# A decoder layer on one core: weight sums moved in GpSimd's order, routers taken in pairs, and four smaller moves

## The chip, the core and the metric

The kernel runs on one core of a Trainium2 chip. The engines run side by side, each in the order of its own queue: TensorE (PE in the profile; PEld is its loading of weights), VectorE (DVE), ScalarE (ACT), GpSimd (POOL), and SyncE (SP), which here only issues DMAs. ScalarE issues DMAs too. The metric is device time in microseconds (us). Lower is better.

## The reference

x has shape (32, 64, 512), so there are 2048 tokens of 512 elements, seen as 16 tiles of 128 tokens; ctx_1024 is (32, 64, 128). Everything is in 32-bit floats.

```python
x = x + attn(layernorm(x))        # 32 heads of 128, rmsnorm on q and k, with weights and biases
x = x + xattn(layernorm(x), ctx)  # 64 channels: q, k, v, skip are 64x64 products
x = x + ffn(layernorm(x))         # router of 64 experts, the top 8, expert biases

# ffn
logits = einsum('th,eh->te', flat, router_weight) + router_bias      # 512 -> 64
scores = softmax(logits);  topk_w, topk_idx = top_k(scores, 8)
w_sum = topk_w.sum(-1);    w_dense = zeros(T, 64) with topk_w at topk_idx
out = flat * w_sum + w_dense @ expert_bias                           # 64 -> 512
```

In the attention the sequence is 64 tokens long for each of 32 rows, and its weights Wq, Wk, Wv are 512 x 4096, Wo is 4096 x 512.

## The kernel before

**Products by Strassen.** The big products are made of seven block products instead of eight, at one level or two. For this, sums of blocks are wanted on both sides. *Weights* (`Weights.sums`, L114 to L127; `more_sums`, L129 to L155): two VectorE or GpSimd subtractions t1, t2 (768 columns, L120), then two more on GpSimd, then for the second level four of 512 and four of 384 columns (L152 to L155). It is a generator with a `yield` after each of the four portions. `sums_of_next(n)` starts it for the weights of the next group, and each `make(1)` runs one portion, always on GpSimd. *Tokens* (`AttentionInput.turn`, L339; `inner_input`, L368): VectorE adds L372 and L373, GpSimd adds L375 and L376.

**The attention's loop.** 32 groups (n = 0 to 31) are 16 pairs of heads (hg) times two halves of the tokens. For hg = 0 (n = 0 and 16) a group is two `single` units, one after the other, because the second level's token sums aren't there yet; each runs through the steps of `HeadGroup.project`, and a dictionary from step to function says what is issued behind which step. All other groups are one `Window` of two units, with a plan of 4 x 4 places (n, m), to which `more` adds. Behind step 6 and step 11 of a single unit, and at set places of a window, `line.scale` multiplies earlier queries and keys by fetched inverse roots: the key part at once on GpSimd (L572), the query part a little later on VectorE (L574). `line.attend` then makes the scores s (L585), which need both, and the mixtures o.

**Order.** TensorE follows the order of the program text everywhere; VectorE, ScalarE and GpSimd follow it too during the attention. So an instruction that is issued earlier in the text stands ahead of all that follow on its engine. After the attention a scheduler places the instructions of those three engines, while TensorE's order stays as written. PSUM tiles rotate: three for projections (`ps_a`), two for transposes and values (`ps_t`), three for scores, keys and router logits (`ps_s`).

**The tail.** The output product goes through the tiles in pairs of a Strassen step (`strassen_out`), in chunks of eight TensorE passes. After each chunk `advance()` moves the tiles on that wait for cross attention and experts, each a generator (`after_attention`) whose `yield k` says how many chunks to let pass. `cross_attention` loads the context (L1090), makes keys and values `kv` (L1094, L1095), energies `e` (L1105), probabilities, their transposes and `py` (L1114, L1149). `experts` makes the transposed input `ft`, the logits `pl` (L1173), the largest eight and the dense weights `wds` on VectorE, the transposed weights `pw`, and the mixtures `pm` (L1222), added at L1225. Two tiles share `pw` and the mixtures already; each has its own logits. `layernorm` (L266) takes the inverse root on GpSimd, except for the last tile's, which ScalarE makes.

**Other lines touched.** `normed_tile` (L1326) normalises a tile of the second half in three steps, of which the third is VectorE's L1328 and a store. `load_wo` (L846) loads blocks of Wo; for the first of them two go through SP's queue ahead of the last window, and two through ScalarE's at place (1, 0).

Of the kernel before, what the change touches and what calls it, by code (L numbers as in the profile page):

```python
# [13 lines left out]
P = 128  # L14
# [27 lines left out]
def decoder_layer(  # L42
# [202 lines left out]
    def fill_behind(t, what):  # L245
        if (t, what) in FILL:
            fill(FILL[t, what])

    def statistics(xs, name, on_gpsimd=False):

        n = len(xs)
        mv = small.tile([P, n, 2], F32, tag=f"mv{n}", name=f"mv_{name}")
        for i, xt in enumerate(xs):
            st = small.tile([P, 6], F32, tag="st", name=f"st{i}_{name}")
            nc.vector.bn_stats(st, xt)
            nc.vector.bn_aggr(mv[:, i, :], st)
        rstd = small.tile([P, n], F32, tag=f"rs{n}", name=f"rs_{name}")
        if on_gpsimd:
            nc.gpsimd.tensor_scalar(rstd, mv[:, :, 1], LN_EPS, None, ALU.add)
            nc.gpsimd.tensor_tensor(rstd, rstd, mhalf[:, 0:n], ALU.pow)  # L260
        else:
            nc.scalar.activation(rstd, mv[:, :, 1], AF.Ln, bias=ln_eps)
            nc.scalar.activation(rstd, rstd, AF.Exp, scale=-0.5)
        return [(mv[:, i, 0:1], rstd[:, i : i + 1]) for i in range(n)]

    def layernorm(xt, name):  # L266
        ((mean, rstd),) = statistics([xt], name, not name.endswith(str(NT - 1)))
        xn = work.tile([P, D], F32, tag="xn", name=f"xn_{name}", bufs=3)
        nc.vector.tensor_scalar(xn, xt, mean, rstd, ALU.subtract, ALU.mult)
        return xn  # L270
# [572 lines left out]

    def load_wo(k, n, places, queue):  # L846

        halves = []
        for i, it in enumerate(places):
            it = it.rearrange("p (g f) -> p g f", f=DH)  # L850
            queue.dma_start(
                out=it,
                in_=wo.rearrange("(g k p) f -> k p g f", k=HG, p=HD)[
                    k, :, i * KH : (i + 1) * KH, bass.ts(n, DH)
                ],
            )
            halves.append(it)
        return halves
# [225 lines left out]
    def cross_attention(t, xt, apart):  # L1084
# [2 lines left out]

        name = f"x{t}"
        ct = work.tile([P, MCTX], F32, tag="ct", name=f"ct_{t}")
        nc.sync.dma_start(out=ct, in_=ctx_flat[bass.ts(t, P), :])  # L1090
        xn = layernorm(xt, name)
        yield 1
        kv = ps_s.tile([P, 2, MCTX], F32, tag="ps", name=f"kv_{t}")
# [68 lines left out]
    def experts(t, xt):  # L1162
        name = f"f{t}"
        xn = layernorm(xt, name)

        yield 8 if t == NT - 2 else 3
        ft = work.tile([P, KC, P], F32, tag="ft", name=f"ft_{name}", bufs=1)
        nc.scalar.copy(ft, transposed(xn.rearrange("p (kc k) -> p kc k", k=P), name))
        fill_behind(t, "router's input")
        yield 1  # L1170
        pl = ps_s.tile([P, NEXP], F32, tag="ps", name=f"pl_{name}")
        for kc in range(KC):
            nc.tensor.matmul(  # L1173
                pl, ft[:, kc, :], rwt[:, kc, :], start=kc == 0, stop=kc == KC - 1
            )
        fill_behind(t, "router")
        lg = work.tile([P, NEXP], F32, tag="lg", name=f"lg_{name}")
        nc.vector.tensor_tensor(lg, pl, rb_b, ALU.add)
        top = small.tile([P, 8], F32, tag="top", name=f"top_{name}")
        nc.vector.max(top, lg)  # L1180
        neg = small.tile([P, 1], F32, tag="neg", name=f"neg_{name}")
        nc.vector.tensor_scalar(neg, top[:, 0:1], -1.0, None, ALU.mult)
        ex = work.tile([P, NEXP], F32, tag="ex", name=f"ex_{name}")
        den = small.tile([P, 1], F32, tag="den", name=f"den_{name}")
        nc.scalar.activation(ex, lg, AF.Exp, bias=neg, accum_out=den)
        inv = small.tile([P, 1], F32, tag="inv1", name=f"inv1_{name}")
        nc.vector.reciprocal(inv, den)

        rest = work.tile([P, NEXP], F32, tag="rest", name=f"rest_{name}")
        nc.vector.match_replace(rest, top, lg, -3e38)  # L1190
        chosen = work.tile([P, NEXP], F32, tag="chosen", name=f"chosen_{name}")
        nc.vector.tensor_tensor(chosen, lg, rest, ALU.not_equal)

        alone = t >= NT - 2
        side = 0 if alone else t % 2
        if side:
            wds, other = chosen_by.pop(t - 1)
        else:
            wds = work.tile([P, 2, NEXP], F32, tag="wds", name=f"wds_{name}")
        wd = wds[:, side, :]  # L1200
        nc.vector.scalar_tensor_tensor(wd, ex, inv, chosen, ALU.mult, ALU.mult)
        ws = small.tile([P, 1], F32, tag="ws", name=f"ws_{name}")
        nc.vector.tensor_reduce(ws, wd, AX.X, ALU.add)

        nc.vector.scalar_tensor_tensor(xt, xn, ws, xt, ALU.mult, ALU.add)
        if not alone and not side:
            chosen_by[t] = wds, xt
            return
        yield 3
        n = NEXP if alone else 2 * NEXP  # L1210
        pw = ps_t.tile([P, P], F32, tag="pt", name=f"pw_{name}")
        nc.tensor.transpose(pw[0:n, :], wds.rearrange("p a e -> p (a e)")[:, 0:n], ident)
        wt = work.tile([P, P], F32, tag="wt", name=f"wt_{name}")
        nc.scalar.copy(wt[0:n, :], pw[0:n, :])
        fill_behind(t, "weights")
        yield 1

        both = [(t, xt)] if alone else [(t - 1, other), (t, xt)]
        pms = [ps_a.tile([P, D], F32, tag="pa", name=f"pm{i}_{name}") for i in range(len(both))]
        for i, pm in enumerate(pms):  # L1220
            rows = slice(i * NEXP, (i + 1) * NEXP)
            nc.tensor.matmul(pm, wt[rows, :], eb_sb[rows, :], start=True, stop=True)  # L1222
        fill_behind(t, "experts")
        for (at, it), pm in zip(both, pms):
            nc.vector.tensor_tensor(it, it, pm, ALU.add)  # L1225
            nc.sync.dma_start(out=out_flat[bass.ts(at, P), :], in_=it)

# [150 lines left out]
    def make(count):  # L1378
        for _ in range(count):
            if making and next(making[0], making) is making:  # L1380
                making.pop()

    for n, (hg, half) in enumerate(groups):
# [3 lines left out]
        if hg == 0:  # L1387
# [2 lines left out]
                {  # L1390
                    3: lambda: coming[0].norm(),
                    6: lambda: (coming.pop(0).turn(), coming[0].norm()),
                    11: lambda: coming.pop(0).turn(),
                },
            )
# [7 lines left out]
            def inner(o):  # L1403
                next(inners[o], None)

            sums_of_next(n)
            make(1)
            single(
                units[1],
                {  # L1410
# [3 lines left out]
                    4: lambda: inner(5),  # L1414
                    6: lambda: (make(1), inner(2)),
                    8: lambda: inner(6),
                    11: lambda: make(2),
                    12: lambda: inner(7),
                },
            )  # L1420
        else:
            more = {
                (0, 3): [lambda n=n: sums_of_next(n), lambda: make(1)],
                (1, 0): [lambda: make(1)],
                (1, 3): [lambda: make(1)],
                (3, 0): [lambda: make(2)],
            }

            def also(n, m, it):
                more.setdefault((n, m), []).append(it)  # L1430
# [11 lines left out]
                    also(*at, lambda o=o: inner(o))  # L1442
            if half == 0 and 2 <= hg < 2 + NT // 2:
                norm = normed_tile(NT // 2 + hg - 2)
                for at in ((0, 0), (0, 3), (1, 2)):
                    also(*at, lambda norm=norm: next(norm, None))
            if (hg, half) == (NHG - 1, 0):

# [7 lines left out]

            if n + 1 == len(groups):
                four = four_blocks("wo_0")
                wo_b = [[load_wo(0, 0, four[0:2], nc.sync)], []]
                also(1, 0, lambda: wo_b[1].append(load_wo(1, 0, four[2:4], nc.scalar)))  # L1460
                a_0 = [[None, None], [None, None]]

                def mixture(t, h, place):
                    a_0[t][h] = load_mixed(t, h, place())

                def qk_buffer(name):
                    return work.tile([P, BLK], F32, tag="qk", name=name, bufs=4)
# [177 lines left out]
```

## Time and profile before

| | |
|---|---|
| median of 3 runs | 1870.45 us (1868.06 to 1873.12) |
| profiled execution | 1869.75 us |
| its span | 1868.0 us (1.75 us around it) |
| granted TensorE clock | 0.999 |
| busy: PE, PEld, DVE, ACT, POOL | 1850.4, 1616.9, 1245.1, 653.6, 1014.7 us |
| PE p_w L685 (second-level projections) | 721.1 us in 2940 passes |
| POOL L120 (first-level weight sums) | 249.7 us in 126 |

The profile is one execution. A timeline line gives the start, the time, the engine, the source line, the operation with what it writes and reads, and in brackets the idle time ahead of it with what ended it. A line of the waits gives who waited for whom, the sum, the number of times and the longest. A product of 32-bit floats shows as two passes of TensorE; a pass's own duration overlaps the next one's, so passes are costed by the distance of their starts.

### The profile page before, as it was taken

Reading aid. Unit: us, or ns where it says so; the run is one execution under the profiler, and the core shown is the slowest. Engines: PE = TensorE matmul, PEld = TensorE weight load, DVE = VectorE, ACT = ScalarE, POOL = GpSimd, SP = SyncE. Lnnn points to the kernel's source line nnn. Section 1 sums busy time; section 2 is a strip of 40 time slices with the busy share of each in tenths; the row PEclk is TensorE's granted clock in tenths of the full one; section 3 lists DMA queues with packets and bytes.
Section 4 is the critical chain, followed back from the end, with each engine's and each line's share of the span. In section 5 each row is a group of like instructions: output and inputs, shape, how many; then the busy total and the mean of one; then the engine's idle time right before and its main releaser. Section 6 shows DMA issues by size and latency. Waiting matters only on the chain.

```text
span 1868.0 us, 40676 instructions
## 1 busy us (share of the span) xinstructions
PE 1850.4 (99%) x16914; PEld 1616.9 (87%) x16914; DVE 1245.1 (67%) x2110; ACT 653.6 (35%) x1577; POOL 1014.7 (54%) x852
## 2 busy tenths in 40 slices
PE   9999999999999999999999999999999999999999
PEld 8888998898899888898889988988888888788876
DVE  6877777777666758777667767766684445554555
ACT  2344444444433443434443343444312202221222
POOL 4866777776667639776667777766242121212120
PEclk9999999999999999999999999999999999999999
DMA  4234434433443343333343333334944231223100
GB/s 143 69 122 144 134 125 131 131 109 110 131 136 114 114 139 112 109 109 103 130 134 123 109 110 114 103 115 141 312 122 159 91 116 68 71 94 116 46 26 23
DMA packets 164650, 215.06 MB, mean 115 GB/s; under 512 B 10161, under 2 KB 135153, under 8 KB 160369
## 3 DMA queue, kind: packets, MB, share of 16 engines
q1 hardware_dynamic: 157648, 206.62, 34.2%
q10 hardware_dynamic: 6816, 5.83, 1.0%
q8 instruction: 133, 2.18, 0.5%
q14 instruction: 53, 0.43, 0.1%
HBM read 172.05 MB, written 40.37 MB: 114 GB/s over the span
## 4 chain that ended last, share of the span: by engine, by line
PE 88%; DVE 4%; DMA 3%; POOL 3%; ACT 1%; issue 1%; SPq 0%; ACTq 0%; POOLq 0%; DVEq 0%
PE p_w L685 32%; PE py L879 17%; PE va L417 11%; PE vb L417 8%; PE o L622 3%; PE s L585 3%; PE ms_w L821 3%; PE pt_p L279 1%; PE pa L475 1%; PE e_x L1105 1%; PE py_x L1149 1%; PE pt_x L279 1%; POOL w L120 1%; PE pl_f L1173 1%; PE py_x L1114 1%; PE pb L475 1%
## 5 line engine op out<-in xcount | busy, mean ns | idle before, releaser
L685 PE MATMUL p_w<-x,w 128*128 128x256 f32 x2940 | 721.1, 382 | 2.5 <-DVE qk L696 1.7
L685 PEld LDWEIGHTS p_w<-x,w 128*128 128x128 f32 x2940 | 521.4, 190 | 59.3 <-DVE qk L696 1.2
L417 PEld LDWEIGHTS va<-w,x 128*128 128x128 f32 x2048 | 268.6, 192 | 13.0
L696 DVE TENSOR_TENSOR qk<-p_w,qk 128x512 f32<-128x512 f32 x360 | 213.1, 599 | 94.6 <-PE p_w L685 92.3
L433 ACT COPY v<-va 128x256 f32<-128x256 f32 x256 | 96.2, 376 | 497.5 <-PE va L417 497.5
L417 PE MATMUL va<-w,x 128*128 128x128 f32 x2048 | 269.9, 275 | 0.0
L709 DVE TENSOR_TENSOR qk<-p_w,qk 128x512 f32<-128x512 f32 x360 | 220.5, 620 | 46.5 <-PE p_w L685 43.1
L120 POOL TENSOR_TENSOR w<-w 128x768 f32<-128x768 f32 x126 | 249.7, 1993 | 2.4
L572 POOL TENSOR_TENSOR qk<-qk,rs 128x512 f32<-128x512 f32 x128 | 173.0, 1352 | 111.8 <-DMA rs<-row_w 99.4
L295 POOL TENSOR_TENSOR prob<-prob,inv 128x512 f32<-128x512 f32 x64 | 79.2, 1237 | 281.5 <-DVE inv L294 278.3
L879 PE MATMUL py<-wo,a 128*128 128x256 f32 x992 | 227.2, 382 | 0.0
L386 ACT ACTIVATE sq<-qk 128x512 f32<-128x512 f32 x256 | 161.4, 631 | 183.6 <-DVE qk L709 64.4
L879 PEld LDWEIGHTS py<-wo,a 128*128 128x128 f32 x992 | 184.1, 190 | 32.9 <-issue 8.6
L417 PEld LDWEIGHTS vb<-w,x 128*128 128x128 f32 x1536 | 201.3, 192 | 9.7
L417 PE MATMUL vb<-w,x 128*128 128x128 f32 x1536 | 202.4, 275 | 0.0
L574 DVE SCALAR_TENSOR_TENSOR qk<-qk,gqk,rs 128x512 f32<-128x512 f32 x128 | 164.7, 1287 | 3.8 <-DMA rs<-row_w 3.5
L879 PE MATMUL py<-wo_t,a 128*128 128x256 f32 x672 | 155.1, 382 | 0.0
L879 PEld LDWEIGHTS py<-wo_t,a 128*128 128x128 f32 x672 | 124.3, 190 | 18.2 <-issue 1.6
L1003 POOL TENSOR_TENSOR x<-x,p 128x256 f32<-128x256 f32 x42 | 42.9, 1043 | 166.7 <-ACT p L1056 72.2
L437 DVE TENSOR_TENSOR v<-vb,v 128x256 f32<-128x256 f32 x192 | 80.9, 421 | 57.0 <-ACT v L433 28.8
L765 POOL TENSOR_TENSOR qk<-qk 128x256 f32<-128x256 f32 x120 | 102.8, 857 | 10.5 <-DVE qk L709 5.8
L287 DVE TENSOR_REDUCE mx<-s 128x8 f32<-128x512 f32 x64 | 44.1, 689 | 85.4 <-PE s L585 85.3
(197 smaller groups left out, 2253.7 us busy)
## 6 DMA issues: line engine op xcount, KB each, us to landing
rs<-row_w SPq DMA_DIRECT2D x120, 512.0 KB
mixed<-ot SPq DMA_DIRECT2D x64, 512.0 KB
a<-mixed SPq DMA_DIRECT2D x32, 1024.0 KB
w<-in_wq_dram SPq DMA_DIRECT2D x64, 256.0 KB
w<-in_wk_dram SPq DMA_DIRECT2D x62, 256.0 KB
w<-in_wv_dram SPq DMA_DIRECT2D x62, 256.0 KB
x<-in_x_dram SPq DMA_DIRECT2D x20, 256.0 KB
rs<-row SPq DMA_DIRECT2D x8, 512.0 KB
```

The lines of the kernel that those rows point to most:

```text
L120: on.tensor_tensor(*(it.rearrange("p c j d -> p (c j) d") for it in (out, a, b)), ALU.subtract)
L386: nc.scalar.activation(sq, of, AF.Square)
L417: nc.tensor.matmul(to[:, j, :], left[i][:, c, j, :], right[i][:, c, 2, :], start=first and j == 0 and c == 0, stop=c == 1, skip_group_chec ...
L433: nc.scalar.copy(self.v[h, ab], what)
L437: nc.vector.tensor_tensor(it, what, it, ALU.add)
L572: nc.gpsimd.tensor_tensor(k, k, rk, ALU.mult)
L574: lambda: nc.vector.scalar_tensor_tensor(q, q, gqk, rq, ALU.mult, ALU.mult)
L685: nc.tensor.matmul(bank[:, s, :], self.w.inner[o][i], inner_x[self.half, o][i], start=first and s == 0, stop=True, skip_group_check=True,)
L696: nc.vector.tensor_tensor(to(t, j), bank, add(t, j), ALU.add)
L709: nc.vector.tensor_tensor(to(t, j), bank, to(t, j), ALU.add)
L765: on.tensor_tensor(to, to, what, ALU.add)
L879: nc.tensor.matmul(py, a[:, g, :], b[g // KH][:, g % KH, :], start=n == 0 and g == 0, stop=n == last and g == NHG - 1,)
```

## The change

1. In the single units, `sums_of_next(n)` and the first `make(1)` move from between the units to step 9 of unit 0, and `make(2)` (the 384-column sums, and the end of the generator) from step 11 of unit 1 to step 9.
2. In the windows of hg = 1 (n = 1 and 17) the four `make` places move from (0,3), (1,0), (1,3), (3,0) to (1,3), (2,1), (2,3), (3,1). Other windows keep theirs.
3. For hg = 2 the third step of `normed_tile` moves from (1,2) to (2,2).
4. The routers of tiles 0 to 13 are taken in pairs. Both inputs lie in one tile `fts`; the router's weights are now the stationary operand, 64 columns for each of the two tiles in turn, and the logits of both come out transposed in `plt`; ScalarE copies them to `lgt` and one transpose makes `pl` for both. VectorE adds the bias for both in one instruction, and then makes the two tiles' weights one after the other. Tiles 14 and 15 stay alone, as before.
5. The inverse root of x13, x15 and f15 is made by ScalarE (before: x15 and f15).
6. The contexts of tiles 0 and 1 are loaded through ScalarE's queue.
7. The first four blocks of Wo are all loaded through ScalarE's queue, one at each of (0,2), (1,0), (1,2), (1,3) of the last window.

```diff
+    on_scalar = (f"x{NT - 3}", f"x{NT - 1}", f"f{NT - 1}")
+
     def layernorm(xt, name):
-        ((mean, rstd),) = statistics([xt], name, not name.endswith(str(NT - 1)))
+        ((mean, rstd),) = statistics([xt], name, name not in on_scalar)
...
-        nc.sync.dma_start(out=ct, in_=ctx_flat[bass.ts(t, P), :])
+        (nc.scalar if t < 2 else nc.sync).dma_start(out=ct, in_=ctx_flat[bass.ts(t, P), :])
...
+        alone = t >= NT - 2
+        if alone or t % 2 == 0:
+            fts = work.tile([P, 2, KC, P], F32, tag="att", name=f"ft_{name}", bufs=1)
+        else:
+            fts, x_a, xn_a = chosen_by.pop(t - 1)
+        ft = fts[:, 0 if alone else t % 2, :, :]
...
+        elif t % 2 == 0:
+            chosen_by[t] = fts, xt, xn
+            return
         else:
...
+            tiles = [(t - 1, x_a, xn_a), (t, xt, xn)]
+
+            plt = ps_s.tile([P, P], F32, tag="ps", name=f"plt_{name}")
+            for kc in range(KC):
+                for side in range(2):
+                    nc.tensor.matmul(
+                        plt[side * NEXP : (side + 1) * NEXP, :],
+                        rwt[:, kc, :],
+                        fts[:, side, kc, :],
+                        start=kc == 0,
+                        stop=kc == KC - 1,
+                    )
+            lgt = work.tile([P, P], F32, tag="wt", name=f"lgt_{name}")
+            nc.scalar.copy(lgt, plt)
+            yield 0
+            pl = ps_s.tile([P, 2, NEXP], F32, tag="ps", name=f"pl_{name}")
+            nc.tensor.transpose(pl.rearrange("p a e -> p (a e)"), lgt, ident)
...
-        yield 3
-        n = NEXP if alone else 2 * NEXP
+        yield 3 if alone or t == 1 else 2
+        n *= NEXP
...
                     6: lambda: (coming.pop(0).turn(), coming[0].norm()),
+                    9: lambda n=n: (sums_of_next(n), make(1)),
                     11: lambda: coming.pop(0).turn(),
...
-            sums_of_next(n)
-            make(1)
...
                     8: lambda: inner(6),
-                    11: lambda: make(2),
+                    9: lambda: make(2),
                     12: lambda: inner(7),
...
+            at = ((0, 3), (1, 0), (1, 3), (3, 0)) if hg > 1 else ((1, 3), (2, 1), (2, 3), (3, 1))
             more = {
-                (0, 3): [lambda n=n: sums_of_next(n), lambda: make(1)],
-                (1, 0): [lambda: make(1)],
-                (1, 3): [lambda: make(1)],
-                (3, 0): [lambda: make(2)],
+                at[0]: [lambda n=n: sums_of_next(n), lambda: make(1)],
+                at[1]: [lambda: make(1)],
+                at[2]: [lambda: make(1)],
+                at[3]: [lambda: make(2)],
             }
...
-                for at in ((0, 0), (0, 3), (1, 2)):
+                for at in ((0, 0), (0, 3), (1, 2) if hg > 2 else (2, 2)):
...
-                wo_b = [[load_wo(0, 0, four[0:2], nc.sync)], []]
-                also(1, 0, lambda: wo_b[1].append(load_wo(1, 0, four[2:4], nc.scalar)))
+                wo_b = [[[]], [[]]]
+                for i, at in enumerate(((0, 2), (1, 0), (1, 2), (1, 3))):
+                    also(
+                        *at,
+                        lambda i=i: load_wo(
+                            i // 2, 0, four[i : i + 1], nc.scalar, wo_b[i // 2][0]
+                        ),
+                    )
```

More of the change, by code (lines that the diff above doesn't have):

```diff
@@ L842, in deviations, with load_wo @@
                     next(it, None)
-    def load_wo(k, n, places, queue):
-        halves = []
-        for i, it in enumerate(places):
+    def load_wo(k, n, places, queue, halves=None):
+        halves = [] if halves is None else halves
+        for it in places:
+            i = len(halves)
             it = it.rearrange("p (g f) -> p g f", f=DH)
@@ L1166, in experts @@
         yield 8 if t == NT - 2 else 3
-        ft = work.tile([P, KC, P], F32, tag="ft", name=f"ft_{name}", bufs=1)
+        alone = t >= NT - 2
[4 more added lines that the diff above has]
+        ft = fts[:, 0 if alone else t % 2, :, :]
         nc.scalar.copy(ft, transposed(xn.rearrange("p (kc k) -> p kc k", k=P), name))
@@ L1170, in experts @@
         yield 1
[L1171 to L1197, printed above, removed]
-        else:
-            wds = work.tile([P, 2, NEXP], F32, tag="wds", name=f"wds_{name}")
-        wd = wds[:, side, :]
-        nc.vector.scalar_tensor_tensor(wd, ex, inv, chosen, ALU.mult, ALU.mult)
@@ L1202, in experts @@
[L1202 to L1208, printed above, removed]
-        yield 3
-        n = NEXP if alone else 2 * NEXP
+        if alone:
+            tiles = [(t, xt, xn)]
+            pl = ps_s.tile([P, 1, NEXP], F32, tag="ps", name=f"pl_{name}")
+            for kc in range(KC):
+                nc.tensor.matmul(
+                    pl[:, 0, :], ft[:, kc, :], rwt[:, kc, :], start=kc == 0, stop=kc == KC - 1
+                )
+            fill_behind(t, "router")
+        elif t % 2 == 0:
+            chosen_by[t] = fts, xt, xn
+            return
+        else:
+            tiles = [(t - 1, x_a, xn_a), (t, xt, xn)]
+            plt = ps_s.tile([P, P], F32, tag="ps", name=f"plt_{name}")
+            for kc in range(KC):
+                for side in range(2):
+                    nc.tensor.matmul(
+                        plt[side * NEXP : (side + 1) * NEXP, :],
[9 more added lines that the diff above has]
+            nc.tensor.transpose(pl.rearrange("p a e -> p (a e)"), lgt, ident)
@@ new lines, in experts @@
+        n = len(tiles)
+        lgs = work.tile([P, n, NEXP], F32, tag="lg", name=f"lg_{name}")
+        nc.vector.tensor_tensor(
+            lgs, pl, rb_b.unsqueeze(1).to_broadcast([P, n, NEXP]), ALU.add
+        )
+        wds = work.tile([P, n, NEXP], F32, tag="wds", name=f"wds_{name}")
+        for side, (at, x_, xn_) in enumerate(tiles):
+            lg = lgs[:, side, :]
+            top = small.tile([P, 8], F32, tag="top", name=f"top{side}_{name}")
+            nc.vector.max(top, lg)
+            neg = small.tile([P, 1], F32, tag="neg", name=f"neg{side}_{name}")
+            nc.vector.tensor_scalar(neg, top[:, 0:1], -1.0, None, ALU.mult)
+            ex = work.tile([P, NEXP], F32, tag="ex", name=f"ex{side}_{name}")
+            den = small.tile([P, 1], F32, tag="den", name=f"den{side}_{name}")
+            nc.scalar.activation(ex, lg, AF.Exp, bias=neg, accum_out=den)
+            inv = small.tile([P, 1], F32, tag="inv1", name=f"inv1{side}_{name}")
+            nc.vector.reciprocal(inv, den)
+            rest = work.tile([P, NEXP], F32, tag="rest", name=f"rest{side}_{name}")
+            nc.vector.match_replace(rest, top, lg, -3e38)
+            chosen = work.tile([P, NEXP], F32, tag="chosen", name=f"chosen{side}_{name}")
+            nc.vector.tensor_tensor(chosen, lg, rest, ALU.not_equal)
+            wd = wds[:, side, :]
+            nc.vector.scalar_tensor_tensor(wd, ex, inv, chosen, ALU.mult, ALU.mult)
+            ws = small.tile([P, 1], F32, tag="ws", name=f"ws{side}_{name}")
+            nc.vector.tensor_reduce(ws, wd, AX.X, ALU.add)
+            nc.vector.scalar_tensor_tensor(x_, xn_, ws, x_, ALU.mult, ALU.add)
@@ L1216, in experts @@
         yield 1
-        both = [(t, xt)] if alone else [(t - 1, other), (t, xt)]
-        pms = [ps_a.tile([P, D], F32, tag="pa", name=f"pm{i}_{name}") for i in range(len(both))]
+        pms = [ps_a.tile([P, D], F32, tag="pa", name=f"pm{i}_{name}") for i in range(len(tiles))]
         for i, pm in enumerate(pms):
@@ L1223, in experts @@
         fill_behind(t, "experts")
-        for (at, it), pm in zip(both, pms):
+        for (at, it, _), pm in zip(tiles, pms):
             nc.vector.tensor_tensor(it, it, pm, ALU.add)
@@ L1458, in decoder_layer @@
                 four = four_blocks("wo_0")
-                wo_b = [[load_wo(0, 0, four[0:2], nc.sync)], []]
-                also(1, 0, lambda: wo_b[1].append(load_wo(1, 0, four[2:4], nc.scalar)))
+                wo_b = [[[]], [[]]]
[5 more added lines that the diff above has]
+                        ),
+                    )
                 a_0 = [[None, None], [None, None]]
```

## The prediction

> **What bounds the kernel now.** I read the page's table of engines and its chain first, then TensorE's list of waits, then the timelines of the places that the diff touches.
>
> ```profile
> PE 1850.4 (99%) x16914; PEld 1616.9 (87%) x16914; DVE 1245.1 (67%) x2110; ACT 653.6 (35%) x1577; POOL 1014.7 (54%) x852
> PE 88%; DVE 4%; DMA 3%; POOL 3%; ACT 1%; issue 1%; SPq 0%; ACTq 0%; POOLq 0%; DVEq 0%
> ```
>
> TensorE (PE) bounds it, at a granted clock of 0.999, and idles only 1868.0 − 1850.4 = 17.6 us. So the change is worth what it takes out of TensorE's instructions, plus the stalls that it removes, less those that it makes. The list of waits says where the stalls are:
>
> ```profile
> PE kv L1094 <- DMA ct<-in_ctx_dram: 2.2, 1, 2.2
> PE p_w L685 <- DVE qk L696: 1.7, 2, 0.9
> PE pa L475 <- DVE qk L490: 0.8, 2, 0.6
> PE pm_f L1222 <- DVE x L1225: 0.8, 1, 0.8
> PE e_x L1105 <- ACT prob_x L1129: 0.6, 1, 0.6
> PE s L585 <- POOL qk L572: 0.4, 1, 0.4
> PE p_w L685 <- POOL x L375: 0.2, 1, 0.2
> ```
>
> GpSimd (POOL) looks half idle over the span; in the first stretches of each half (34 to 95 and 699 to 764 us) it is the full engine. From 40 to 62 us it is busy for 19.05 of 22 us, without a gap from 38.65 to 59.0:
>
> ```profile
> 52.89 1.45 POOL L572 TENSOR_TENSOR qk<-qk,rs 128x512 f32<-128x512 f32 x1
> 54.30 1.00 POOL L152 TENSOR_TENSOR w<-w 128x384 f32<-128x384 f32 x1
> ...
> 57.82 1.18 POOL L155 TENSOR_TENSOR w<-w 128x384 f32<-128x384 f32 x1
> ...
> 721.14 1.72 POOL L572 TENSOR_TENSOR qk<-qk,rs 128x512 f32<-128x512 f32 x1
> 722.82 1.19 POOL L152 TENSOR_TENSOR w<-w 128x384 f32<-128x384 f32 x1
> ...
> 726.18 1.00 POOL L155 TENSOR_TENSOR w<-w 128x384 f32<-128x384 f32 x1
> ```
>
> And TensorE beside it, in its timelines:
>
> ```profile
> 56.14 1.15 PE L585 MATMUL s<-qk 128*64 128x64 f32 x32
> ...
> 722.91 0.92 PE L585 MATMUL s<-qk 128*64 128x64 f32 x24 [0.41 <-POOL qk L572]
> 738.27 1.97 PE L685 MATMUL p_w<-x,w 128*128 128x256 f32 x8 [0.92 <-DVE qk L696]
> 759.28 0.92 PE L685 MATMUL p_w<-x,w 128*128 128x256 f32 x3 [0.21 <-POOL x L375]
> 1442.50 1.08 PE L1149 MATMUL py_x<-att_x,kvs 128*64 128x512 f32 x4
> 1457.30 1.00 PE L1173 MATMUL pl_f<-rwt,ft_f 128*128 128x64 f32 x8
> 1458.14 1.95 PE L879 MATMUL py<-wo,a 128*128 128x256 f32 x8
> ```
>
> To see: the scores s need the second k scaling L572, at 722.91 they already wait for it, and what stands next on POOL are four sums of 384 columns.
>
> **VectorE beside GpSimd.** A VectorE operation with both inputs in SBUF waits out the running POOL instruction:
>
> ```profile
> 65.71 0.41 DVE L372 TENSOR_TENSOR x<-x 128x256 f32<-128x256 f32 x1
> ...
> 40.52 1.82 DVE L372 TENSOR_TENSOR x<-x 128x256 f32<-128x256 f32 x1
> ```
>
> At 40.52 POOL ran L120 (40.25 to 44.0). That is the cost the move aims at.
>
> **The change part by part** (times of before's clock; + is slower).
>
> 1. *First sums (t1, t2) at step 9 of unit 0, n = 0 and 16.* In n = 0 the two L120 (3.71 us at 34.58) come to 25.9, behind L362 that ends at 25.86. The loads of those weights move no bytes after about 22, so they hold nothing. The order put POOL's next L361 at 33.08, free. But VectorE's L333 (0.55 at 26.39) then waits to about 27.8, L490 (26.85) ends near 28.6 rather than 27.5, and TensorE's product at 28.06 needs that bank: +0.6 (0 to 1.2). Nothing returns at 38.65: L375 waited there for L372, which waits for a TensorE product. In n = 16 the pair moves from 699.55 to 690.5, delays one L572 to 695.5 (used by s at 699.9), and POOL was idle from 703.26 to 705.80 for the softmax anyway: 0.
>
> 2. *The 384 sums at step 9 of unit 1, not 11.* Step 11 also issues the k scaling, and issued it first. Now the four sums precede the second L572. n = 0: start 52.89, sums 4.7 (54.30 to 59.0), scaling 1.27 to 1.45: done at 59.0, and s, whose ninth pass was at 56.41, stalls +2.6 (1.3 to 3.0). A stall of 0.35 (0.5 in start-to-start excess) at 60.45 behind VectorE's L706 goes: −0.5. n = 16: 721.14 + 4.36 + 1.27 to 1.72 = 726.8 to 727.2 against 722.9: +4.1 (3.5 to 4.6). Nothing covers these: behind s stand o and p_w in TensorE's own order.
>
> 3. *Window n = 1 and 17, all sums a quarter later.* The first L120 pairs leave the stretch of L372/L373 and L574; the stall at 738.27 (0.92, by start-to-start excess 1.08) and 0.18 at 755.29 go: −1.2 (0 to −1.3), n = 17 alone. In exchange the second L120 pair stands between two pairs of L765. In n = 1: softmax scaling done at 83.6, L765 pair when VectorE's L709 ends at 84.3 (two of 0.79), L120 3.6 to 4.2, L765 pair, L375 0.73: ends 91.9 to 92.6, where L375 ended at 90.62 and p_w started upon it at 90.68: +1.5 (0.5 to 2.5), and the same in n = 17 at 759.28: +1.5. The 384 sums end near 102; the next window needs the first at about 100.5 and has it at 98.9: 0.
>
> 4. *hg = 2: third step of the normalising at (2,2).* L1328 (1.87 at 116.39, beside POOL) leaves the chain that ends in stalls at 120.83, 124.52 (0.80) and 127.52: −1.2 (−1.4 to +0.3). The store of the normalised tile, on SP's queue, is later by the same stretch; its reader is hundreds of us away.
>
> Parts 1 to 4: 0.6 + 2.6 − 0.5 + 4.1 − 1.2 + 3.0 − 1.2 = **+7.4**.
>
> 5. *Routers in pairs, 7 pairs.* Two groups of 8 passes of 64 columns go, 1457.30 to 1458.14 = 0.84 each, 1.68. In come 16 passes with 64-column weights in two column halves, 128 columns moving, and one transpose. The nearest row is py_x (128*64): of its four passes two start at 1442.50 and two at 1442.98, side by side. A 128-column pass takes 0.109 (transposes start that far apart), so 8 × 0.109 = 0.87, plus 0.15 for entering and leaving (py_x paid 0.09 twice), plus 0.11: 1.13. −0.55 × 7 = **−3.8**. Fully side by side without switching gives −4.9; one after the other, 16 × 0.109 + 0.11 = 1.86, +1.3. ScalarE's added copy (0.3) has a py chunk of 1.73 as cover; VectorE's two chains need about 5.9 of 7.0 us in most pairs. In f13, with statistics between them, the cover is short: +0.2 (0 to 1).
> [...]
>
> 6. *f1.* pm1 waits for L1225 to read pm0 (0.78). In the new order that read stands behind two reciprocals and normalisations (prob_x) on VectorE: +0.8 (0 to 1.2).
>
> 7. *x13's rstd on ScalarE.* POOL's 2.16 us at 1786 leaves the chain to e_x at 1793.62: −0.8 (0 to −0.9).
>
> 8. *First contexts.* SP issued ct_0 at 1407.61, behind three `a` loads that held it for 9.5 us; it landed at 1418.1, kv idled 2.15. ScalarE's queue issues at about 1408.5, behind eb's packets that move until 1416.2: landing near 1416.9, −1.2 (−2.2 to +1). SP's next two `a` loads go 4 us earlier and share the engines.
>
> 9. *wo_0 in four pieces on ScalarE's queue.* SP's L851, which waited for TensorE with row_w and rs behind it, is gone; the first use is 60 us later. −0.2 (−1 to +2, if ScalarE waits at an issue and its copies of va with it).
>
> Sum: 7.4 − 3.8 + 0.2 + 0.8 − 0.8 − 1.2 − 0.2 = **+2.4 us**, on the profiled execution's 1869.75 (span 1868.0 and 1.75 around it): 1872.2. It lies 0.70 below the median of 1870.45, so I forecast **1872.9**.
>
> **Rivals.** A change under 5.6 us (0.3%) is about what this kernel's times can't tell from none.
> (a) *Slower*: routers don't overlap. Then +1.3 replaces −3.8, and the total is +7.5, 1878; it decides once the pair of halves costs over 1.6 us. The 0.643 us of a py_x pass against 0.592 later hints at some cost; the equal starts speak against it.
> (b) *Faster*: the room that the first L120 pairs leave lets POOL's chain move up, so that the scaling of part 2 is done in time although the sums stand before it. The chain would have to start 2.6 us (n = 0) and 4.1 us (n = 16) earlier than now. Without those 6.7 us the sum is −4.3, and with routers at −4.9 and contexts at −2.2 it is −6.4: 1864. For it speaks that POOL is busy with that pair right ahead of the chain; against it, that the chain's first instructions wait for VectorE's L372 (ends 38.57) and the softmax's reciprocal (705.42), and that it has no gap from there to 721.14.
> (c) *The change does nothing by its sums*: order alone, each stall replaced by an equal one; only routers −3.8 and contexts −1.2: 1865.5. Against it, the order listed above.
>
> **How the numbers follow.** Forecast's case (between −5.6 and +5.6) 0.50; slower by more 0.34, which is (a) with full stalls, or window sums at their upper bounds; faster by more 0.16, (b) and the tail of (c). The lower bounds of all terms together make −6.4, the upper ones +20; the terms are independent, so 8 in 10 reach from 1864 to 1881; the likeliest case's own range is 1866 to 1876.
>
> **What would show it.** s at about 59 and 727 waiting for L572 by 2.6 and 4.1; p_w near 92 and 762 waiting for L375 by 1.5; no stall near 738 and 124.5; plt's passes starting in pairs 0.109 apart; kv's wait near 1. Wrong if s doesn't wait, or if the plt passes start one by one.

## The result, and the profile after

The changed kernel takes 1881.10 us (median of 5 runs, 1876.72 to 1885.15) against 1870.45 us of before (median of 5, 1868.03 to 1873.12). The ratio is 1.0054, with a 95% interval of 1.0041 to 1.0067, so it is about 10 us slower. The profiled execution took 1877.91 us with a span of 1876.1 us, 8.1 us over the span before. The stated range is 1864 to 1881, and the time stands at its upper end: the median is a tenth of a microsecond past it, the ratio just inside (1881 would be 1.0056). The forecast of 1872.9, inside 0.3%, was not the case that came; that was the slower one, given 34%.

Two views of the changed kernel say where the time went: the page's row of engines and its list of TensorE's waits (who waits for whom: us in total, times, longest).

```profile
PE 1846.5 (98%) x16921; PEld 1610.8 (86%) x16921; DVE 1246.3 (66%) x2103; ACT 656.1 (35%) x1586; POOL 1008.2 (54%) x850
```

```profile
PE s L588 <- POOL qk L575: 10.1, 3, 4.6
PE p_w L688 <- POOL x L378: 4.5, 2, 2.9
...
PE pm_f L1250 <- DVE x L1253: 1.3, 1, 1.3
```

TensorE is busy for less, 1846.5 instead of 1850.4 us, yet idles for 29.6 (1876.1 − 1846.5) instead of 17.6 us. The waits of s went from 0.4 to 10.1, those of p_w for the token sums from 0.2 to 4.5; kv's wait of 2.2 and e_x's of 0.6 are not in the list any more. (Lines of after are three or four higher up to the experts: L572 is L575 now, L375 is L378.)

GpSimd's timeline at the first of the s waits, and at the p_w wait of n = 17, with TensorE's in a fence of its own:

```profile
52.40 1.18 POOL L152 TENSOR_TENSOR w<-w 128x384 f32<-128x384 f32 x1
...
56.03 1.18 POOL L155 TENSOR_TENSOR w<-w 128x384 f32<-128x384 f32 x1
57.17 1.44 POOL L575 TENSOR_TENSOR qk<-qk,rs 128x512 f32<-128x512 f32 x1
...
759.74 1.35 POOL L298 TENSOR_TENSOR prob<-prob,inv 128x512 f32<-128x512 f32 x1 [4.87 <-ACT ot L640]
761.05 1.26 POOL L575 TENSOR_TENSOR qk<-qk,rs 128x512 f32<-128x512 f32 x1
762.28 1.98 POOL L768 TENSOR_TENSOR qk<-qk 128x256 f32<-128x256 f32 x2
764.22 3.76 POOL L120 TENSOR_TENSOR w<-w 128x768 f32<-128x768 f32 x2
767.94 1.71 POOL L768 TENSOR_TENSOR qk<-qk 128x256 f32<-128x256 f32 x2
769.61 0.90 POOL L378 TENSOR_TENSOR x<-x 128x256 f32<-128x256 f32 x1
```

```profile
58.67 1.43 PE L588 MATMUL s<-qk 128*64 128x64 f32 x24 [2.58 <-POOL qk L575]
60.03 3.08 PE L688 MATMUL p_w<-x,w 128*128 128x256 f32 x8
...
731.60 1.55 PE L588 MATMUL s<-qk 128*64 128x64 f32 x24 [4.58 <-POOL qk L575]
...
770.57 1.13 PE L688 MATMUL p_w<-x,w 128*128 128x256 f32 x4 [2.91 <-POOL x L378]
...
1379.85 1.55 PE L588 MATMUL s<-qk 128*64 128x64 f32 x24 [2.90 <-POOL qk L575]
```

The four 384-column sums stand ahead of the key scaling, and s waits 2.58 and 4.58 us for it, where the steps said 2.6 and 4.1. At 60.03 there is something that no step held: eight passes of p_w take 3.08 us, and the same eight took 1.99 before:

```profile
57.22 1.99 PE L685 MATMUL p_w<-x,w 128*128 128x256 f32 x8
```

The windows of the changed kernel's trace show why. Each row has the stretch and its length, the busy time and the count of instructions of PE, PEld, DVE, ACT and POOL, the granted clock (PEclk, 1.00 is full), and the DMA's share and GB/s:

```profile
58.84:62.25 3.41, 3.41 (x29) 2.92 (x28) 1.49 (x3) 0.63 (x1) 0.00 (x0) 0.50 0.85 246
62.25:65.66 3.41, 3.41 (x21) 3.08 (x20) 2.07 (x4) 1.21 (x3) 1.77 (x3) 1.00 0.76 250
731.27:734.68 3.41, 3.08 (x84) 2.97 (x88) 1.38 (x2) 0.00 (x0) 0.27 (x1) 0.50 0.58 161
734.68:738.09 3.41, 3.41 (x35) 3.08 (x28) 1.49 (x4) 3.21 (x8) 0.35 (x1) 1.00 1.05 346
1379.80:1383.21 3.41, 3.36 (x88) 3.16 (x88) 3.31 (x4) 0.00 (x0) 3.28 (x1) 0.50 0.48 153
```

Behind each of the three s waits TensorE runs at half its clock for 3.41 us. Before had one such stretch, at 10.7 us while the kernel starts. (Both traces have one more at the very end, when nothing is left to do, at 1867.56 and 1874.73.)

**Where the 8.1 us of span come from.** I took the start of the same matmul in both traces and noted where the difference jumps. Positive is later in the changed kernel.

| place (before's clock) | jump, us | the step's value |
|---|---|---|
| start-up, half-clock stretch at 10.7 not there | −0.9 | not in it |
| 28.06, bank behind L490; 45.28, the same | +0.6 −0.2 | +0.6 |
| 56.4 s, and 60.45 | +2.8 −0.5 | +2.6 −0.5 |
| 722.9 s | +4.2 | +4.1 |
| 90.7 p_w, n = 1 | +1.6 | +1.5 |
| 738, 755 and 759 p_w, n = 17 | −1.3 +2.7 | −1.2 +1.5 |
| 121 to 127.5, and va at 132 | −1.4 +1.0 | −1.2 |
| half clock behind the s waits, 3 times | +4.4 | not in it |
| 1341 ms_w; 1367 s in the drain (the last groups, where the output product begins) | −1.0 +2.9 | −0.2 |
| 1418 kv | −2.3 | −1.2 |
| routers, f1's pm, x13 | −3.2 +0.5 −1.1 | −3.8 + 0.2 + 0.8 − 0.8 |

These make +8.8; small shifts between these places, about 0.2 or less each, add up to some −0.6, and the whole is +8.2.

### The profile page after: what moved, and what is told of

It reads as the page before. It is cut to its first block, busy times and chain, and to the rows that moved or that the text cites. A ratio compares the mean times of both kernels' runs of the same rounds, so it can differ in the third digit from the quotient of the medians.

```text
span 1876.1 us, 40697 instructions
## 1 busy us (share of the span) xinstructions
PE 1846.5 (98%) x16921; PEld 1610.8 (86%) x16921; DVE 1246.3 (66%) x2103; ACT 656.1 (35%) x1586; POOL 1008.2 (54%) x850
## 4 chain that ended last, share of the span: by engine, by line
PE 91%; POOL 4%; DMA 2%; DVE 1%; issue 1%; ACT 1%; SPq 0%; POOLq 0%; ACTq 0%; DVEq 0%
PE p_w L688 33%; PE py L883 20%; PE va L420 11%; PE vb L420 8%; PE o L625 4%; PE s L588 4%; PE ms_w L824 3%; PE pt_p L282 1%; POOL w L120 1%; PE e_x L1109 1%; PE py_x L1153 1%; PE pa L478 1%; PE pt_x L282 1%; PE py_x L1118 1%; POOL qk L575 1%
## 5 line engine op out<-in xcount | busy, mean ns | idle before, releaser
L575 POOL TENSOR_TENSOR qk<-qk,rs 128x512 f32<-128x512 f32 x128 | 172.4, 1348 | 106.7 <-DMA rs<-row_w 85.5
L577 DVE SCALAR_TENSOR_TENSOR qk<-qk,gqk,rs 128x512 f32<-128x512 f32 x128 | 168.8, 1319 | 4.1 <-DMA rs<-row_w 4.1
L768 POOL TENSOR_TENSOR qk<-qk 128x256 f32<-128x256 f32 x120 | 103.8, 865 | 11.1 <-DVE qk L712 6.4
```

Source lines behind the costliest of these rows:

```text
L575: nc.gpsimd.tensor_tensor(k, k, rk, ALU.mult)
L577: lambda: nc.vector.scalar_tensor_tensor(q, q, gqk, rq, ALU.mult, ALU.mult)
L768: on.tensor_tensor(to, to, what, ALU.add)
```

## The experiments

All times are ratios to the kernel before on the same chip. "Alone" means the kernel before with one part of the change.

**1. The sums back at step 11** (e1), the rest of the change kept.

```diff
-                    9: lambda: make(2),
+                    11: lambda: make(2),
```

> The changed kernel with the 384-column sums back at step 11 of the second single unit, behind the key scaling. Theory (order on GpSimd, and the clock that falls after a long TensorE stall): the waits of s on the key scaling near 58.7 (2.58) and 731.6 us (4.58) go, 0.4 remains at the second; the two half-clock stretches of 3.41 us behind them go as well, 1.7 us each. The stall of 0.5 behind L709 near 60 us returns. Against the changed kernel's profile: -2.6 -4.2 -3.3 +0.5 = about -9.6 us, some 1866 to 1868 of span. Rival (only the stalls' own length counts, the granted clock is the chip's mood): about -6.3 us and half-clock stretches still there, elsewhere. Rival (the chain on GpSimd moves elsewhere and the stalls return): under 2 us.

Ratio 1.0029 (1.0018 to 1.0041), median 1874.92, profiled span 1869.4. Both waits of s in the single units are gone but for 0.42 us, and so are the half-clock stretches behind them. The profile is 6.7 us shorter than the changed kernel's, not 9.6: another half-clock stretch stands at 762.13, behind the 2.9 us wait of p_w, where the changed kernel had none behind a wait of the same length, and the wait in the drain is 3.47. The ratio fell by 0.0025, about 5 us.

**2. The same step alone** (e10): the kernel before with the sums at step 9.

```diff
-                    11: lambda: make(2),
+                    9: lambda: make(2),
```

> The kernel before with the 384-column sums at step 9 instead of 11 of the second single units, and nothing else. Theory: s waits 2.6 and 4.6 us for the key scaling, -0.5 near 60 us, and the half clock adds 1.4 to 1.6 after the second always and after the first when its idling lies in one grid stretch: 2.6 + 4.2 - 0.5 + 1.4 to 3.0 = +7.7 to +9.3 in the attention, of which up to 2 us come back at the wait of kv, as the transfers go on meanwhile: +6 to +8.5 us, ratio 1.0032 to 1.0045. Rival (the stalls are made by the first portion's move, not by this one): under +2 us.

Ratio 1.0055 (1.0043 to 1.0068). This one line makes as much as the whole change. TensorE's timeline of this kernel:

```profile
60.29 1.55 PE L585 MATMUL s<-qk 128*64 128x64 f32 x24 [2.57 <-POOL qk L572]
...
732.06 1.36 PE L585 MATMUL s<-qk 128*64 128x64 f32 x24 [4.59 <-POOL qk L572]
```

The stalls have the lengths of the changed kernel, and half-clock stretches begin at 59.91 and 732.34. The rival, that the first portion's move makes them, falls. The time is over my 6 to 8.5 us: the profiled span of 1879.5 also holds a p_w wait of 0.8 at 75.8, a wait of s in the drain of 1.3, and a start-up that is 1.1 longer than before's.

**3. The later places of hg 1 alone** (e8).

```diff
+            at = ((0, 3), (1, 0), (1, 3), (3, 0)) if hg > 1 else ((1, 3), (2, 1), (2, 3), (3, 1))
```

> The kernel before with the later places of hg 1's weight sums and nothing else. Theory: p_w waits for L375 by 1.7 near 91 and 2.9 near 761 (there one more key scaling of 1.27 stands between the softmax and the sums), the stalls near 738 and 755 go (-1.4): +1.5 +2.7 -1.4 = +2.8 us, and +1.6 more in those runs in which the second stall falls into one grid stretch. Rival (the waits appeared only because the other changes had delayed GpSimd): -1.4 us.

Ratio 1.0016 (1.0007 to 1.0024), so +3.0 us where +2.8 was expected. The waits are 1.63 near 92 and 2.95 at 761.87; the stall at 738 is gone. A wait of s in the drain, 1.92, with a half-clock stretch behind it, is there too. This run and the first one give the sharpest look at the clock: the same wait of p_w, in e8 and in e1, a timeline line and a window of each.

```profile
761.87 1.13 PE L685 MATMUL p_w<-x,w 128*128 128x256 f32 x4 [2.95 <-POOL x L375]
...
762.13:765.54 3.41, 3.41 (x25) 3.20 (x25) 2.56 (x6) 1.46 (x4) 3.25 (x4) 1.00 0.00 0
```

```profile
762.06 2.05 PE L688 MATMUL p_w<-x,w 128*128 128x256 f32 x4 [2.93 <-POOL x L378]
...
762.13:765.54 3.41, 3.41 (x12) 3.06 (x13) 2.21 (x4) 0.46 (x1) 3.25 (x4) 0.50 0.00 0
```

After 2.95 us of idling 25 passes go at full clock, after 2.93 us 12 at half. So the length of a stall alone doesn't decide. The first wait of s shows the same: in e2 (below), which has the changed kernel's order there, it is 2.58 us as well, and no half clock follows it.

```profile
58.86 0.92 PE L588 MATMUL s<-qk 128*64 128x64 f32 x24 [2.58 <-POOL qk L575]
...
60.83:64.24 3.41, 3.41 (x22) 3.10 (x21) 2.59 (x5) 1.73 (x4) 1.23 (x2) 1.00 0.84 230
```

**4. A ladder of stalls** (e4): the kernel before with twelve added stalls of TensorE of growing length; it ran once.

```diff
+    STEPS = (2, 5, 7, 9, 10, 11, 12, 13, 14, 16, 20, 28)
+    chain = const.tile([P, 64], F32, tag="chain", name="chain")
+
+    def idle(steps, hg):
+        pt = ps_t.tile([P, P], F32, tag="pt", name=f"pt_c{hg}")
+        nc.tensor.transpose(pt, ident, ident)
+        nc.scalar.copy(chain, pt[:, 0:64])
+        for _ in range(steps):
+            nc.scalar.copy(chain, chain)
+        pt = ps_t.tile([P, P], F32, tag="pt", name=f"pt_d{hg}")
+        nc.tensor.transpose(pt[0:64, :], chain, ident)
...
+            if half == 0 and 3 <= hg < 15:
+                also(0, 0, lambda hg=hg: idle(STEPS[hg - 3], hg))
```

> The kernel before with twelve added stalls of TensorE, one at the start of each window of hg 3 to 14 of the first half: a transpose, a chain of 3 to 29 small ScalarE copies in place, and a transpose that needs the last; about 0.9 to 6 us of idling. Theory (the clock is set by how much TensorE idled in a fixed stretch of 3.41 us): no half clock after a stall under 1.7 us, always one after stalls over about 5 us, and in between it depends on how the stall lies to the grid of 3.41 us: a grid stretch that idled 75% or more is followed by 3.41 us of half clock that costs 1.7 us, one that idled 55% or less is not. Rival (length of the stall alone): one threshold, about 2.5 us, whatever the place in the grid. Rival (the half clock belongs to the s and o matmuls after the stall): none in this run. The time grows by the sum of the stalls plus 1.7 us for each half-clock stretch.

The stalls came out longer than meant, 1.28 to 8.49 us. The first ones in TensorE's timeline, and two windows:

```profile
188.22 0.30 PE L1379 MATMUL pt_d<-ident,chain 128*64 128x128 f32 x1 [2.12 <-ACT chain L1377]
232.43 0.42 PE L1379 MATMUL pt_d<-ident,chain 128*64 128x128 f32 x1 [2.67 <-ACT chain L1377]
278.60 0.30 PE L1379 MATMUL pt_d<-ident,chain 128*64 128x128 f32 x1 [3.22 <-ACT chain L1377]
```

```profile
279.68:283.09 3.41, 3.41 (x14) 3.06 (x13) 1.38 (x2) 0.00 (x0) 3.33 (x3) 0.50 0.47 162
283.09:286.50 3.41, 3.41 (x21) 3.10 (x20) 2.67 (x4) 0.37 (x1) 3.41 (x3) 1.00 0.00 0
```

After 1.28 and 2.12 us there is no half clock: eight passes of p_w go at 0.22 from start to start there (188.35 to 190.08 behind the second). The other ten have it, with passes 0.43 apart, for 3.41 us, or for 6.83 and once 10.24 us where the stall goes on into the next stretch of the grid described here. No s or o follows these stalls, so they aren't what it belongs to. The half-clock stretches of a trace begin a whole number of 3.413 us apart: in the changed kernel 731.27 − 58.84 = 197 and 1379.80 − 731.27 = 190 of them, in e10 732.34 − 59.91 = 197, in e9 1482.69 − 1417.84 = 19. Laid on that grid, the stall of 2.12 was split into 1.42 and 0.69, and the one of 2.67 put 2.13 into one stretch. In e2 the wait of 2.58 lies across two stretches that idle 1.14 and 1.44 of 3.41. Of the grid stretches at full clock in this run, those that the stalls of 2.67 to 4.61 us left idle for 2.13 to 2.39 us (62% to 70%) were followed by half clock; those idle for 1.28, 1.42 and, ahead of the 2.39 of the stall of 4.34, 1.95 us (57%) were not. In the changed kernel those with the three s waits idled 2.58, 3.41 and 2.85 us (76%, 100%, 84%) and were followed by it; the wait of p_w of 2.91 lies across two, 1.15 and 1.76 (51%), and neither was. Away from the pm matmuls (below), these two traces don't contradict my bounds of 55% and 75%. Behind a stretch at half clock less was enough: in this run those that idled 1.26 (stall of 3.51), 1.50, 1.72, 1.89 and 2.41 us were each followed by another.

**5. The changed kernel again** (e11), without an edit.

> The changed kernel itself once more, for a second profile and times. Theory (free-running grid): the stalls keep their places and lengths (s 2.6 and 4.6, p_w 1.6 and 2.9), the half-clock stretch behind the 4.6 us stall is there, those behind 2.6 and 2.9 come and go with the place of the grid; the wait of s in the drain differs by a microsecond or more, as it depends on transfers. Rival (stall and clock are bound to the program alone): the same three stretches at the same places.

Ratio 1.0055 (1.0038 to 1.0073). The waits are 2.57, 4.59, 1.65 and 2.94, and 3.06 in the drain. Half-clock stretches stand behind the same three s waits and a fourth behind f1's pm at 1496.55. By start times of the same matmuls, the two traces part by 1.3 us at 1383 to 1385 and by 1.7 us at 1494 to 1496, where six and eight passes each take 0.43 instead of 0.22: its third stretch lasts 6.83 us, and the fourth is not in the other trace. Why the third goes on is open: its first 3.41 us idled only 0.74. In the five runs of the result, span and mean granted clock go together: 1874.9 and 1876.1 us at 0.997, 1879.2 and 1879.9 at 0.995, 1883.4 at 0.994. A stretch lowers the mean by 0.5 × 3.41 / 1876 = 0.0009, so this is a spread of about three stretches, some 4 to 5 of the 8.5 us between the shortest and the longest span. The two profiles of the same program have three and, counting the long one twice, five of them. That the drain's wait differs by over a microsecond was wrong for this pair, 2.90 and 3.06.

**6. Wo's blocks**, put back in the changed kernel (e2), and moved alone (e7).

```diff
-                wo_b = [[[]], [[]]]
...
+                wo_b = [[load_wo(0, 0, four[0:2], nc.sync)], []]
+                also(1, 0, lambda: wo_b[1].append(load_wo(1, 0, four[2:4], nc.scalar)))
```

> The changed kernel with the first four blocks of Wo loaded as before (two through SP's queue ahead of the last window, two through ScalarE's at place (1,0)). Theory: the wait of s on the key scaling near 1380 us (2.90) comes from the roots' row, written 2.9 us late because SP was held for 6.08 us at the issue of the output bias (4.03 before), behind Wo pieces that were still moving; it goes, with the half-clock stretch behind it: -2.7 -1.5 +1.0 (the small waits near 1341 return) = about -3 us. Rival (the late row comes from the changed order of SP's queue or from the later arrival of the whole stretch, not from Wo's loads): the wait stays, 0 us.

> The kernel before with the first four blocks of Wo through ScalarE's queue, one each at (0,2), (1,0), (1,2), (1,3) of the last window, and nothing else. Theory (this part alone makes the wait of s in the drain): s waits for the key scaling by 2.5 to 3.5 us near 1369, a half-clock stretch behind it if the idling falls into one grid stretch, the small waits near 1341 go (-1), kv's wait shrinks by as much as the delay: the net is +0.5 to +3 us. Rival (the late row in the changed kernel came from the other changes): no wait of s, -1 us.

Put back: ratio 1.0069 (1.0049 to 1.0090), no gain. The wait of s in the drain falls from 2.90 to 0.94 and its half clock goes, but kv then waits 3.21 for ct. Alone: ratio 1.0007 (0.9998 to 1.0016); s waits 3.43 with a half-clock stretch behind it, and kv, which waited 2.15 before, doesn't wait. So what s loses in the drain seems to be largely time in which the contexts land meanwhile. The wait in the drain isn't Wo's alone: it was 0.02 before, 0.68 in e5, 1.33 in e10 and 1.92 in e8, none of which touches Wo. The queue's hold of 6.08 us at the output bias, on which my expectation rested, is in the changed kernel's trace, but it doesn't go with the wait: it is 5.49 in e2, where s waits 0.94, and 5.17 in e7, where s waits 3.43. What sets that wait from kernel to kernel stays open.

**7. The contexts alone** (e5).

```diff
-        nc.sync.dma_start(out=ct, in_=ctx_flat[bass.ts(t, P), :])
+        (nc.scalar if t < 2 else nc.sync).dma_start(out=ct, in_=ctx_flat[bass.ts(t, P), :])
```

> The kernel before with the first two contexts loaded through ScalarE's queue and nothing else. Theory (the context comes no earlier that way: in the changed kernel its issue on ScalarE's queue stood 6.1 us ahead of the first keys, against 8.4 us on SP's before; the 2.6 us won there were the upstream stall's, which left the transfers their time): kv waits for ct by 2 to 4 us, the time is 0 to +2 us against before. Rival (ScalarE's queue brings it earlier): kv's wait under 0.5 us, -1.5 to -2.5 us.

Ratio 1.0000 (0.9990 to 1.0010). kv waits 0.77 and 0.32 in its trace, less than the 2 to 4 expected, but no time is won. With SP's queue the wait was 2.15 in one trace, 0.72 in the next (e3) and 2.01 in another (e9): it varies by more than the move brings.

**8. The routers alone** (e3): the new function `experts` in the kernel before.

> The kernel before with the routers paired and nothing else. Theory: each of seven pairs is 0.46 us shorter (0.84 saved at the first router, 0.38 paid at the pair), the wait for pm of the first pair is 0.5 longer: -3.2 +0.5 = about -2.7 us against before, in profile and in time. Rival (in the changed kernel the tail is shorter for other reasons, the earlier contexts above all): 0 to -1.

Ratio 0.9988 (0.9979 to 0.9997), −2.2 us; the rest of the changed tail isn't needed for it. The changed kernel's timeline shows the pair:

```profile
1474.91 1.09 PE L1198 MATMUL plt_f<-ft_f,rwt 128*64 128x128 f32 x16
1475.93 1.99 PE L883 MATMUL py<-wo,a 128*128 128x256 f32 x8
1477.76 0.27 PE L1209 MATMUL pl_f<-ident,lgt_f 128*128 128x128 f32 x1
1477.87 3.62 PE L883 MATMUL py<-wo,a 128*128 128x256 f32 x16
```

Sixteen passes take 1.02 from start to start, side by side in the two column halves (single records start in twos, 0.006 apart, and 0.109 from two to two), and the transpose 0.11: the 1.13 of the estimate. By start times a pair saves 0.46; the 0.09 that is missing lies ahead of the transpose, where a chunk of 1.73 takes 1.83 (1475.93 to 1477.76).

**9. What paid, without what didn't** (e6, e9): the kernel before with routers, x13 on ScalarE, the normalising step at (2,2), and other places for hg 1's sums. The places of e6, then those of e9:

```diff
+                    (1, 3): [lambda n=n: sums_of_next(n), lambda: make(1)],
+                    (2, 3): [lambda: make(2)],
+                    (3, 1): [lambda: make(2)],
...
+                    (1, 3): [lambda n=n: sums_of_next(n), lambda: make(2)],
+                    (2, 3): [lambda: make(3)],
```

> The kernel before with the parts that paid: routers in pairs, x13's inverse root on ScalarE, the third step of hg 2's normalising at (2,2), and for hg 1 the first portion of weight sums at (1,3), the second and third at (2,3) behind the last token sum, the fourth at (3,1). Theory: routers -2.7, x13 -0.9, normalising -0.45, hg 1 -1.4 (stall near 738) and -0.4 (the waits for L375), none of the waits of s: about -5.5 us, span near 1862 to 1863. Rival (GpSimd's sums are late for the next window instead): stalls of p_w on w near 100 and 768 us, -2 us or less.

> As the kernel of the parts that paid, but for hg 1 with the first and second portion of weight sums both at (1,3), where GpSimd stood idle for five microseconds ahead of the softmax, and the third and fourth at (2,3). Theory: the waits of p_w on w (1.03 near 99.5, 0.38 near 766.5) go and nothing else comes: about -1.5 us against that kernel, -6 to -7 us against before. Rival (the second pair now runs beside VectorE's SBUF sums and delays them): a stall behind L696 or L709 of 0.5 to 1.5 comes back, no gain.

e6: ratio 0.9974 (0.9963 to 0.9985), median 1865.97, with waits of p_w for L152 of 1.03 and 0.38. In e9 these are gone, and the ratio is 0.9975 (0.9965 to 0.9985), median 1865.29: the same within the intervals. Both beat the kernel before by about 5 us, and the changed one by about 15. In e9's profiled execution 1.58 of waiting behind L698 at 1313 and two half-clock stretches, at 1417.84 behind kv's wait and at 1482.69 behind pm, took back what was won in that execution.

## Why the prediction was right or wrong

*First sums at step 9 of unit 0.* Right: the added wait is 0.43, with a jump of 0.59 against +0.6; 0.2 came back at 45.28, where a wait of 0.16 is gone.

*384 sums at step 9 of unit 1.* The mechanism and the lengths were right, +2.8 and +4.2 for +2.6 and +4.1. The step failed in "+2.6" and "+4.1" being the whole price: behind these two stalls the granted clock was 0.50 for 3.41 us, which cost 1.64 and 1.34 by start times, and 1.45 behind the wait in the drain. Alone, this part measures about 10 us where the step had +6.2.

*Window n = 1 and 17.* n = 1 was right to a tenth. For n = 17 the mis-sized term is the second "+1.5", measured +2.7: I carried the list of n = 1 over, and in n = 17 one more key scaling (1.26 at 761.05) stands between the softmax and the L768 pairs. Alone: +3.0 against the step's +1.8.

*hg = 2.* Right in its place, −1.4 for −1.2, but not run alone: in e3, without the step, 0.4 of it is gone too. The va wait of 0.8 at 132 is not this step's: e5, without the step, has one of 0.77 at the same place, and e6 and e9, with it, have none.

*Routers.* 1.13 a pair, as estimated; the saving of a pair is 0.46 rather than 0.55. The old router's passes of 64 columns took 0.105 each (0.84 for eight), nearly the 0.109 of 128 columns. That isn't the price of 64 columns as such, though: 32 passes of s, also 64 columns but with 64-column weights and side by side in twos, take 1.08 from start to start (56.14 to 57.22 before), 0.068 for two. The 0.105 came with 128-column weights; what set it was not tried.

*f1.* The direction was right, +0.5 for +0.8, in this trace. In e3, e9 and e11 a half-clock stretch follows it, which cost 1.7 in e11.

*x13.* −1.1 for −0.8; shown by the traces only, not run alone.

*First contexts.* Wrong: "landing near 1416.9, −1.2". The issue on ScalarE's queue stood 6.1 us ahead of the first kv (1423.71 to 1429.77), on SP's 8.4 us ahead of the time at which kv was due. The 2.3 us at kv in the trace came from upstream: the stall of s in the drain gives the transfers time, as in e7 and e8, where kv doesn't wait although the contexts are on SP's queue. Alone the move is worth nothing.

*Wo in pieces.* The upper bound of +2 was named for ScalarE's copies; what came was a wait in the drain's s, and what that costs comes back at kv.

*The rivals.* (a), "routers don't overlap", ended on the right side by the wrong mechanism: they do overlap. (b) fell: the chain on GpSimd didn't move up; its sums ended at 730.3, the scaling at 731.5. (c) fell with it. That the end of the range meets the time is luck: it was made of the tails of many small terms, and the missing term, the clock, was not among them. In the profile the sum is off by 5.8 us (+8.2 for +2.4); 4.4 of them are the half clock, 1.2 the second wait of p_w, and what else was off nearly cancels. The medians lie 10.65 apart; the profiled execution was one of those with the clock at 0.997, and others had 0.994 and 0.995.

*What stays open.* The parts don't add up: one step alone makes 1.0055, yet taking it out of the change leaves 1.0029. Part of that is the places (+3.0 alone) and the waits near 3 us that are left: the one of p_w fell into one grid stretch in e1's trace (2.93 us, half clock behind it) and across two in the changed kernel's (1.15 and 1.76, full clock). The spread of e1's runs (1870.79 to 1880.78) fits that, but no execution near e1's median was profiled.

## What to carry to other kernels

Look at what is queued ahead of an operand on its engine, not only at which engine is free: GpSimd's four sums of 1.1 us, moved two steps up, stood in front of the one scaling that TensorE was about to need. Here a stall of the bounding engine cost more than its length (1.64 us on top of 2.58, 1.34 on top of 4.58), so check the granted clock right after one. And judge a transfer's gain by running it alone: a wait that vanishes in a trace may only have moved upstream.

## What the runs showed of the hardware that was not expected

TensorE's granted clock was 0.50 for 3.41 us behind each of the changed kernel's three s waits, which had left 2.58, 3.41 and 2.85 us of one stretch of a 3.413 us grid idle. The length of a stall alone didn't tell: 2.58 us (the changed kernel's s) and 2.93 us (e1's p_w), each within one stretch, had it behind them; 2.58 us (e2's s: 1.14 and 1.44) and 2.91 us (the changed kernel's p_w: 1.15 and 1.76), each across two, didn't, nor did 2.95 us (e8's p_w). The price was 1.3 to 1.7 us: the passes in such a stretch went at half speed, the big ones at 0.43 instead of 0.22. Around the pm matmuls less was enough. In e3 the first stretch below idled 1.28 us (38%) by the records, with five passes in it, and the second is at half clock; e9 and e11 show the same, while in e6 such a stretch idled 1.25 us and full clock followed.

```profile
1478.46:1481.87 3.41, 2.13 (x5) 0.54 (x5) 1.67 (x5) 0.60 (x4) 0.00 (x0) 1.00 0.12 45
1481.87:1485.28 3.41, 3.41 (x8) 2.23 (x8) 0.62 (x1) 0.00 (x0) 0.00 (x0) 0.50 0.54 186
```

Why less idling was enough there wasn't tried.
